# Merging four stages of a macaron network into one pipeline over sequences, with the weights rounded during the stage before

## The chip, the cores and the metric

The kernel runs on one core of one Trainium2 chip. Its time is the device time of that core in microseconds (us), from the start of the program to its end. A core has five engines with instruction queues of their own: TensorE (PE, matrix products), VectorE (DVE), ScalarE (ACT), GpSimd (POOL) and SyncE (SP, which here issues the transfers). Each works its queue off in order, and semaphores tie the queues together.

## The reference

A residual network of four layers works on 8 sequences of 512 tokens with 128 features, all in fp32. Each layer has a half-weighted feed-forward, a mixer and the same feed-forward again. The stretch that matters here is layer 2 and the first third of layer 3:

```python
x = x + 0.5 * _L1_ffn_ref(_layernorm(x), ...)   # mixture of 16 experts, 4 of them used
x = x + 0.5 * _L2_ffn_ref(_layernorm(x), L2_ffn_w_gate, L2_ffn_w_up, L2_ffn_w_down)
x = x + _L2_attn_ref(_layernorm(x), L2_attn_ig_w, ..., L2_attn_a_param)
x = x + 0.5 * _L2_ffn_ref(_layernorm(x), L2_ffn_w_gate, L2_ffn_w_up, L2_ffn_w_down)
x = x + 0.5 * _L3_ffn_ref(_layernorm(x), L3_ffn_w1, L3_ffn_b1, L3_ffn_w2, L3_ffn_b2)
x = x + _L3_attn_ref(_layernorm(x), ...)        # causal attention, 16 heads
```

The feed-forward of layer 2 rounds inputs, weights and hidden values to a 4-bit grid, with one scale for each 16 values:

```python
def fp4_quant_dequant(x):                       # blocks of 16 along the last dimension
    scale = maximum(max(abs(xb)) / 6, 1e-12)    # one for each block
    return grid[searchsorted(mid, abs(xb / scale))] * sign(xb) * scale
gate = fp4_linear(x, w_gate); y = fp4_linear(x, w_up)      # 128 -> 352
return fp4_linear(silu(gate) * y, w_down)                  # 352 -> 128
```

The mixer of layer 2 is a linear recurrence over the tokens, with gates `sigmoid(block-diagonal product)`:

```python
log_a = -8 * gate_a * softplus(a_param)
normed_x = x * gate_x * sqrt(clip(1 - exp(2 * log_a), 1e-7))
p = clip(shifted cumprod(exp(log_a)), 1e-7)     # along the tokens
h = p * cumsum(normed_x / p)
```

The feed-forward of layer 3 is `relu(x @ w1 + b1) @ w2 + b2` with 512 hidden values.

## The kernel before

The residuals stay in SBUF for the whole program, as eight tiles `x0` to `x7` of 128 partitions (tokens) by 4 chunks by 128 features. The program is a list of twelve stages (`_STAGES`, L1595), and `_run_stages` (L1612) calls one after the other. Each stage opens its own pools in SBUF and PSUM, loops over the sequences, and ends with the residual add of each (`add_half`, L391, or L1140 in the recurrence). A framework orders the instructions of each engine by priorities that follow the order of emission, subject to the buffers: pools of a stage take the space that the stage before gives back. The exception is the norm: its tiles come from `ln_pool`, which lives for the whole program, so that norms can be made ahead over a stage's border. Weights come by DMA from SP, one packed transfer for a stage (`load`, L261).

The parts that the change touches:

- `norm` (L274) makes the statistics (`bn_stats` L282, `bn_aggr` L283 on DVE), then one over the root by `pow` on POOL (L285, L287), then applies it, either on ACT (L291 and L293, `scalar=True`) or on DVE (L298). `transposed` (L377) turns four chunks on PE (L381) and copies them from PSUM by ACT (L382).
- `fp4` (L967) rounds a tile. DVE finds the largest value of each block (L977), makes the scale and its inverse (L978, L980, L981). POOL multiplies by the inverse (L983). ACT makes a large number of the same exponent (L985), by which DVE rounds in two passes (L986, L987). POOL multiplies by the scale (L988). One such chain goes DVE, POOL, ACT, DVE, POOL.
- `l2_ffn` (L990) rounds and transposes the three weights the first time it runs (copies at L1008 and L1015), then goes over the sequences: `rounded_in` (L1032: norm, rounding, transposition), `gated_half` (L1041) twice, of two token chunks each (products `pg` and `pu`, silu by ACT L1053, product by DVE L1054, rounding), and `rounded_half` (L1058), one half later (transposes L1066, copies by ACT L1067, product `po` with the down weights, add). The stage runs twice.
- `l2_attn` (L1084) makes the softplus of its rate, then goes over all eight sequences three times: norm, transposition and gates (sigmoid L1112, product by POOL L1113); decay (exponential L1116, POOL L1117, DVE L1118, scaling by the rate L1120, a running sum with a floor as a scan L1123, two exponentials L1126 and L1127); and sums (root L1130, POOL L1131, DVE L1133, scan L1135, product L1136, transposes L1139, add L1140). Changes between sigmoid, exponential, root and silu on ACT cost a table load each.
- `l3_ffn` (L1142) has for each sequence norm (apply on DVE), transposition, four products of 128 by 512 with relu on ACT (L1167), four more that add up in PSUM, bias on ACT (L1176), transposes back (L1158) and add.
- `l1_ffn` (L794), the stage ahead, steps through the experts of each sequence in ten steps (`experts`, L853) and takes the routing of the next sequence along (`routed` L821; `ranks` L897, with POOL's comparison at L910). Its shares, transposed as `shareT`, weigh the experts' products. A generator `self.aside` is stepped at each of the ten steps of sequence 1; in the first of the two expert stages it makes constants of the attention. `in_order` (L331) fixes the order of the named engines within a step as it was written.

In all of them `mm` (L272) is the line of every matrix product.

Of the kernel before, what the change touches and what calls it, by code (L numbers as in the profile page):

```python
# [10 lines left out]

# [14 lines left out]
P = 128  # L26
# [175 lines left out]
def _attention_pack(p, wq, bq, wk, bk, wv, bv, wo, bo):  # L202
# [32 lines left out]
    ),  # L235
}


class _Kernel:
# [554 lines left out]
    def l1_ffn(self):  # L794
# [3 lines left out]
        with ExitStack() as s:  # L798
# [10 lines left out]
            for b in range(NB):  # L809
                ahead = self.routed(b + 1) if b + 1 < NB else iter(())  # L810
                experts = self.experts(b)
                for _ in range(10):
                    with self.in_order(*(() if b != 1 else (mybir.EngineType.Pool, mybir.EngineType.DVE))):
                        next(experts)
                        next(ahead, None)
                        if b == 1:
                            next(self.aside, None)
                for _ in ahead:
                    pass
# [147 lines left out]
    def fp4(self, out, v, sb, tag):  # L967

        nc = self.nc
        n = v.shape[1]
        blocks = lambda ap: ap.rearrange("p (k i) -> p k i", i=16)
        spread = lambda ap: ap.unsqueeze(2).to_broadcast([P, n // 16, 16])
        scale = sb.tile([P, n // 16], F32, name=f"{tag}_scale")
        nc.vector.tensor_reduce(scale, blocks(v), AX.X, ALU.max, apply_absolute_value=True)  # L977
        nc.vector.tensor_scalar(scale, scale, 1.0 / 6.0, 1e-12, ALU.mult, ALU.max)  # L978
        inv = sb.tile([P, n // 16], F32, name=f"{tag}_inv")
        nc.vector.reciprocal(inv, scale)  # L980
        nc.vector.tensor_scalar(inv, inv, 2.0**-23 - 1.0, None, ALU.mult)  # L981
        r = sb.tile([P, n], F32, name=f"{tag}_r")
        nc.gpsimd.tensor_tensor(blocks(r), blocks(v), spread(inv), ALU.mult)  # L983
        big = sb.tile([P, n], F32, name=f"{tag}_big")
        nc.scalar.activation(big, r, AF.Abs, scale=2.0**22)  # L985
        nc.vector.scalar_tensor_tensor(r, big, 1.5 * 2.0**22, r, ALU.max, ALU.add)  # L986
        nc.vector.scalar_tensor_tensor(r, big, 1.5 * 2.0**22, r, ALU.max, ALU.subtract)  # L987
        nc.gpsimd.tensor_tensor(blocks(out), blocks(r), spread(scale), ALU.mult)  # L988

    def l2_ffn(self):  # L990
        nc, tc = self.nc, self.tc
        w = lambda n: self.w["l2f", n]
        F = 352
        chunk = self.l2_chunks = [(0, P), (P, P), (2 * P, F - 2 * P)]
        with ExitStack() as s:
            sb = s.enter_context(tc.tile_pool(name="sb", bufs=2))
            ps = s.enter_context(tc.tile_pool(name="ps", bufs=2, space=bass.MemoryType.PSUM))
            if not self.l2w:

                self.load("l2f")  # L1000
                for name in ("w_gate", "w_up"):
                    q = sb.tile([P, 3 * P], F32, name="wq")
                    self.fp4(q, w(name), sb, "w")
                    pt = ps.tile([P, 3 * P], F32, name="mm", bufs=1)
                    for k in range(3):
                        nc.tensor.transpose(pt[:, bass.ts(k, P)], q[:, bass.ts(k, P)], self.ident)
                    self.l2w[name] = self.const.tile([P, F], F32, name=f"{name}T")
                    nc.vector.tensor_copy(self.l2w[name], pt[:, :F])  # L1008
                q = sb.tile([P, F], F32, name="wq")
                self.fp4(q, w("w_down"), sb, "w")  # L1010
                self.l2w["w_down"] = self.const.tile([P, 3, P], F32, name="w_downT")
                pt = ps.tile([P, 3, P], F32, name="mm", bufs=1)
                for k, (at, n) in enumerate(chunk):
                    nc.tensor.transpose(pt[:n, k, :], q[:, at : at + n], self.ident)
                    nc.vector.tensor_copy(self.l2w["w_down"][:n, k, :], pt[:n, k, :])  # L1015


            self.sb, self.ps = sb, ps
            self.seqs = [{} for _ in range(NB)]
            self.rounded_in(0)  # L1020
            last = None
            for b in range(NB):
                for half in range(2):
                    self.gated_half(b, half)
                    if last is not None:
                        self.rounded_half(*last)
                    last = (b, half)
                    if half == 0 and b + 1 < NB:
                        self.rounded_in(b + 1)
            self.rounded_half(*last)  # L1030

    def rounded_in(self, b):  # L1032
        sb, ps = self.sb, self.ps
        flat = "p c d -> p (c d)"
        xn = self.norm(self.x[b], self.ln_pool, scalar=True)
        xq = sb.tile([P, NC, D], F32, name="xq")
        self.fp4(xq.rearrange(flat), xn.rearrange(flat), sb, "x")
        xT = sb.tile([P, L], F32, name="xT")
        self.seqs[b]["xT"] = self.transposed(xq, ps, xT, self.nc.scalar.copy, bufs=1)

    def gated_half(self, b, half):  # L1041
        nc, sb, ps = self.nc, self.sb, self.ps
        q, wT = self.seqs[b], self.l2w
        F = 352
        flat = "p c d -> p (c d)"
        h = sb.tile([P, 2, F], F32, name="h")
        for j in range(2):
            tok = q["xT"][:, bass.ts(2 * half + j, P)]
            pg = ps.tile([P, F], F32, name="pg")
            self.mm(pg, tok, wT["w_gate"])  # L1050
            pu = ps.tile([P, F], F32, name="pu")
            self.mm(pu, tok, wT["w_up"])
            nc.scalar.activation(h[:, j, :], pg, AF.Silu)  # L1053
            nc.vector.tensor_tensor(h[:, j, :], h[:, j, :], pu, ALU.mult)  # L1054
        q[half] = sb.tile([P, 2, F], F32, name="hq")
        self.fp4(q[half].rearrange(flat), h.rearrange(flat), sb, "h")

    def rounded_half(self, b, half):  # L1058
        nc, sb, ps = self.nc, self.sb, self.ps
        q, hq = self.seqs[b], self.seqs[b][half]  # L1060
        if half == 0:
            q["hT"] = sb.tile([P, 3, L], F32, name="hT")
        for k, (at, n) in enumerate(self.l2_chunks):
            pt = ps.tile([P, 2, P], F32, name="ht")
            for j in range(2):
                nc.tensor.transpose(pt[:n, j, :], hq[:, j, at : at + n], self.ident)  # L1066
            nc.scalar.copy(  # L1067
                q["hT"][:n, k, bass.ts(half, 2 * P)], pt[:n].rearrange("p c t -> p (c t)")
            )
        if half == 0:  # L1070
            return
        po = ps.tile([P, NC, P], F32, name="po", bufs=1)
        for c in range(NC):
            for k, (_, n) in enumerate(self.l2_chunks):
                self.mm(
                    po[:, c, :],
                    q["hT"][:n, k, bass.ts(c, P)],
                    self.l2w["w_down"][:n, k, :],
                    start=k == 0,
                    stop=k == 2,  # L1080
                )
        self.add_half(b, po)

    def l2_attn(self):  # L1084

        nc, tc = self.nc, self.tc
        w = lambda n: self.w["l2a", n]
        with ExitStack() as s:  # L1090
            keep = s.enter_context(tc.tile_pool(name="keep", bufs=1))
            sb = s.enter_context(tc.tile_pool(name="sb", bufs=2))
            ps = s.enter_context(tc.tile_pool(name="ps", bufs=2, space=bass.MemoryType.PSUM))
            floor = keep.tile([P, L], F32, name="floor")
            nc.gpsimd.memset(floor, float(np.log(1e-7)))
            ones = keep.tile([P, L], F32, name="ones")
            nc.gpsimd.memset(ones, 1.0)
            rate = keep.tile([P, 1], F32, name="rate")
            self.softplus(rate, w("a_param"), keep)
            nc.vector.tensor_scalar(rate, rate, -8.0, None, ALU.mult)  # L1100
            rate2 = keep.tile([P, 1], F32, name="rate2")
            nc.vector.tensor_scalar(rate2, rate, 2.0, None, ALU.mult)

            gated, decay, left, prefix = [], [], [], []
            for b in range(NB):
                xn = self.norm(self.x[b], self.ln_pool, scalar=True)
                xT = self.transposed(xn, ps, sb.tile([P, L], F32, name="xT"), nc.scalar.copy)
# [491 lines left out]
    "l1_ffn",  # L1599
    "l1_attn",  # L1600
    "l1_ffn",
    "l2_ffn",
    "l2_attn",
    "l2_ffn",
    "l3_ffn",
# [32 lines left out]
```

## Time and profile before

| what | value |
|---|---|
| time, median of 3 runs | 2497.51 us (2494.47 to 2501.63) |
| the profiled execution's own time | 2500.23 us |
| its span | 2498.4 us |
| mean granted TensorE clock | 0.902 |
| TensorE busy | 2142.6 us (86%) |
| VectorE busy | 1665.3 us (67%) |
| ScalarE busy | 1216.5 us (49%) |
| GpSimd busy | 652.5 us (26%) |

The shares are means over twelve stages with different limits; what the change is worth has to be read in its own stretch, from the last residual add of the second expert stage to that of layer 3's first feed-forward. In the lines by group, a row gives line, engine, operation, output and inputs, count, then the busy time in us and the mean of one in ns, then the idle time of the engine ahead of it and what ended it. In the waits, a row gives the engine and line that waited, what it waited for, the total in us, how often, and the longest. In the windows, a row gives the stretch, its length, each engine's busy time with the number of instructions, and the granted clock. In the slices a digit is the busy share of one fortieth of the span, in tenths.

### The profile page before, as it was taken

To read this page: it belongs to the slowest core of one execution; us is meant where nothing else is said; L and a number is where in the kernel's file an instruction comes from. 1 tells how busy PE (TensorE), PEld (TensorE's weight loads), DVE (VectorE), ACT (ScalarE), POOL (GpSimd) and SP (SyncE) were. 2 spreads that over 40 slices of the span, in tenths; PEclk is the share of its full clock that TensorE was granted. 3 is DMA by queue.
4 is the path that set the end of the run, shared out by engine and by line. 5 is a ranking of instruction groups with operands and counts; after the bars stand their busy time and mean duration, and the time that the engine had idled before them with its cause. 6 is when DMAs were issued, how large, how long until landed. Compare 5 with 4: busy or idle time off the path is not lost.

```text
span 2498.4 us, 30167 instructions
## 1 busy us (share of the span) xinstructions
PE 2142.6 (86%) x10907; PEld 1033.5 (41%) x10967; DVE 1665.3 (67%) x3867; ACT 1216.5 (49%) x1791; POOL 652.5 (26%) x922
## 2 busy tenths in 40 slices
PE   7679998889998988899979996762578999999989
PEld 3444444434444333333334443541354444444434
DVE  4566774568768788888358777957884466666611
ACT  3545663323321666777723333455444335555554
POOL 1123443012111011112112114553552113333330
PEclk9779998989996899999979998975888969999999
DMA  3000000000000000000000000000000000000001
GB/s 117 1 1 1 1 1 13 10 0 1 0 1 0 1 1 1 1 1 1 1 7 0 1 1 0 1 1 0 1 1 1 0 1 1 1 1 1 1 1 34
DMA packets 10036, 13.08 MB, mean 5 GB/s; under 512 B 416, under 2 KB 8736, under 8 KB 9760
## 3 DMA queue, kind: packets, MB, share of 16 engines
q1 hardware_dynamic: 7776, 10.11, 1.2%
q8 instruction: 86, 1.41, 0.2%
q10 hardware_dynamic: 2112, 1.05, 0.2%
q14 instruction: 62, 0.51, 0.1%
HBM read 9.06 MB, written 2.10 MB: 4 GB/s over the span
## 4 chain that ended last, share of the span: by engine, by line
PE 63%; DVE 19%; POOL 7%; ACT 7%; issue 4%; DMA 0%; ACTq 0%; DVEq 0%; SPq 0%; POOLq 0%
PE pair L272 11%; PE av L272 8%; PE po L272 7%; PE first L272 7%; PE mm L272 6%; PE pg L272 5%; PE pu L272 4%; DVE max L1393 3%; ACT e L1501 3%; PE ph L272 2%; PE ck L272 2%; PE pr L272 1%; PE pw L272 1%; POOL xn_rstd L287 1%; DVE xn L298 1%
## 5 line engine op out<-in xcount | busy, mean ns | idle before, releaser
L1393 DVE TENSOR_REDUCE max<-first 128x1 f32<-128x512 f32 (+3 forms) x864 | 534.8, 666 | 193.5 <-PE first L272 170.4
L1501 ACT ACTIVATE e<-pair 128x1024 f32<-128x1024 f32 (+3 forms) x512 | 436.8, 865 | 241.7 <-PE pair L272 231.4
L272 PE MATMUL first<-qkT 32*128 32x512 f32 (+3 forms) x1024 | 338.4, 474 | 30.6 <-DVE max L1393 29.4
L272 PE MATMUL pair<-qkT 32*128 32x512 f32 (+3 forms) x1024 | 224.3, 457 | 21.1 <-ACT e L1501 14.3
L272 PE MATMUL av<-e,v 128*32 128x512 f32 (+3 forms) x2048 | 240.2, 539 | 1.0
L872 ACT ACTIVATE act<-pg 128x512 f32<-128x512 f32 x144 | 86.0, 597 | 235.1 <-PE pg L272 188.1
L272 PE MATMUL pair<-mT,max_rows 32*128 32x512 f32 (+3 forms) x1024 | 192.1, 376 | 1.8 <-DVE mT L1435 1.8
L272 PEld LDWEIGHTS pair<-qkT 32*128 32x128 f32 x1024 | 95.8, 186 | 235.4 <-ACT e L1501 132.7
L272 PEld LDWEIGHTS first<-qkT 32*128 32x128 f32 x1024 | 153.1, 198 | 96.3 <-DVE max L1393 87.8
L1503 POOL TENSOR_SCALAR_AFFINE_SELECT e<-e 128x256 f32<-128x256 f32 x256 | 103.4, 407 | 253.1 <-ACT e L1501 252.8
L272 PE MATMUL po<-act,w_moe 128*128 128x512 f32 x288 | 157.4, 632 | 3.0 <-DVE act L881 1.9
L272 PE MATMUL pg<-xT,w_moe 128*128 128x512 f32 x288 | 153.7, 616 | 0.0
L272 PE MATMUL pu<-xT,w_moe 128*128 128x512 f32 x288 | 149.3, 601 | 0.0
L873 DVE TENSOR_TENSOR act<-act,pu 128x512 f32<-128x512 f32 x144 | 98.3, 683 | 49.6 <-PE pu L272 47.3
L1399 POOL COPY copies<-max 128x128 f32<-128x128 f32 x64 | 22.6, 410 | 343.3 <-DVE max L1393 343.3
L272 PEld LDWEIGHTS pair<-mT,max_rows 32*128 32x128 f32 x1024 | 97.4, 189 | 3.6 <-DVE mT L1435 3.3
L881 DVE TENSOR_TENSOR act<-act,pw 128x512 f32<-128x512 f32 x128 | 87.1, 682 | 16.5 <-PE pw L272 15.0
L287 POOL TENSOR_TENSOR xn_rstd<-xn_rs,nhalf 128x4 f32<-128x4 f32 x72 | 77.5, 1077 | 54.1 <-ACT xn L293 35.5
L382 ACT COPY xT<-mm 128x512 f32<-128x512 f32 x80 | 46.0, 584 | 89.0 <-PE mm L381 76.8
L381 PE MATMUL mm<-w_const,xn 128*128 128x128 f32 x256 | 51.4, 318 | 42.2 <-DVE xn L298 24.8
L1360 ACT CAST qkT<-pair 128x1024 fp32r<-128x1024 f32 x64 | 64.8, 1014 | 41.3 <-PE pair L272 40.8
L910 POOL TENSOR_TENSOR ge<-ge,w_moe 128x64 f32<-128x64 f32 (+1 forms) x32 | 42.8, 1337 | 153.8 <-DVE ge L908 153.8
(354 smaller groups left out, 4211.2 us busy)
## 6 DMA issues: line engine op xcount, KB each, us to landing
w_moe<-in_moe SPq DMA_DIRECT2D x1, 2392.0 KB, 13.7
out<-x SPq DMA_DIRECT2D x8, 256.0 KB, 2.3
x<-in_u ACTq DMA_DIRECT2D x4, 256.0 KB, 6.5
x<-in_u SPq DMA_DIRECT2D x4, 256.0 KB, 6.4
w_mixer<-in_l0a SPq DMA_DIRECT2D x1, 960.5 KB, 8.2
w_mixer<-in_l1a SPq DMA_DIRECT2D x1, 769.0 KB, 4.2
w_ffn<-in_l0f SPq DMA_DIRECT2D x1, 578.0 KB, 7.3
w_ffn<-in_l2f SPq DMA_DIRECT2D x1, 560.0 KB, 3.5
```

What stands on the lines that cost most here:

```text
L272: self.nc.tensor.matmul(out, lhsT, rhs, start=start, stop=stop)
L287: nc.gpsimd.tensor_tensor(rstd, rs, self.nhalf[:, :n], ALU.pow)
L381: self.nc.tensor.transpose(pt[:, c, :], xn[:, c, :], self.ident)
L382: copy(out, pt.rearrange("p c t -> p (c t)"))
L872: nc.scalar.activation(act, pg, AF.Silu)
L873: nc.vector.tensor_tensor(act, act, pu, ALU.mult)
L881: nc.vector.tensor_tensor(act, act, pw[e % 2], ALU.mult)
L910: nc.gpsimd.tensor_tensor(ge.rearrange(flat), ge.rearrange(flat), self.wide(before, m), ALU.mult)
L1360: self.nc.scalar.copy(t, p)
L1393: nc.vector.tensor_reduce(mx[:, c, j, gs[0] : gs[-1] + 1], sc, AX.X, ALU.max, negate=True)
L1501: nc.scalar.activation(e[:, :, :n], sc[:, :, :n], AF.Exp, scale=scale)
L1503: nc.gpsimd.affine_select(e[:, :, :P], e[:, :, :P], pattern=[[0, 2], [1, P]], compare_op=ALU.is_ge, fill=0.0, base=0, channel_multiplier=-1,)
```

## The change

The four stages `l2_ffn`, `l2_attn`, `l2_ffn` and `l3_ffn` become one, `layer2`. Each sequence's work in each of them is cut into pieces, and every piece has a slot, a number that only orders them. A sequence b's first rounded feed-forward lies at 5.5 b, its recurrence, which goes by pairs of sequences, at 7 + 8 b for the odd b, its second rounded feed-forward at 32 + 8 b, and its relu feed-forward at 40 + 8 b. The pieces are emitted by rising slot.

```diff
+_STARTS = (0, 7, 32, 40)
+_STEPS = (5.5, 8, 8, 8)
+_ROUNDED_FFN = {
+    "stats": -9, "apply": -5, "x_in": -5, "x_out": -4, "turned": -1.5,
+    "gated": (0.5, 0.5, 1, 1), "h_in": (0.5, 2.5), "h_out": (2, 4),
+    "h_turned": (3.5, 5), "down": 7,
+}
+_RECURRENCE = {
+    "stats": -1, "apply": 2, "turned": 2, "gates": 3.5, "decays": 4, "exps": 4,
+    "roots": 4.5, "sums": 5.5, "added": 6.5,
+}
+_RELU_FFN = {
+    "stats": 0.5, "apply": 0.5, "turned": 2, "wide": (3.5, 3.5, 4, 4), "product": 5.5, "added": 10,
+}
...
+    def layer2(self):
...
+            for b in range(NB):
+                put(_STEPS[0] * b, self.rounded_ffn(b))
+                put(_STEPS[2] * b + _STARTS[2], self.rounded_ffn(b))
+                put(_STEPS[3] * b + _STARTS[3], self.relu_ffn(b))
+                if b % 2:
+                    put(_STEPS[1] * b + _STARTS[1], self.recurrence((b - 1, b)))
+            for _, piece in sorted(todo, key=lambda t: t[0]):
+                piece()
```

PSUM has two banks each of `pg`, `pu` and `mm`, which the kinds of piece share, and one each of `ht` and `po`. The norms (`front`) take their tiles from the stage's pool and are all applied on ACT:

```diff
+        def stats():
+            st = sb.tile([P, NC, 6], F32, name=f"{tag}_st")
...
+            nc.gpsimd.tensor_tensor(t["rstd"], rs, self.nhalf[:, :NC], ALU.pow)
+        def apply():
...
+            nc.vector.scalar_tensor_tensor(off, mv[:, :, 0], -1.0, rstd, ALU.mult, ALU.mult)
+            for c in range(NC):
+                nc.scalar.activation(xn[:, c, :], x[:, c, :], AF.Identity, ...)
```

The rounding is cut in two pieces, works in place, and two of its small instructions take a tile of constants as a second input:

```diff
-        nc.vector.tensor_scalar(scale, scale, 1.0 / 6.0, 1e-12, ALU.mult, ALU.max)
+        nc.vector.scalar_tensor_tensor(
+            scale, scale, 1.0 / 6.0, self.least[:, :m], ALU.mult, ALU.max
+        )
...
-        nc.vector.tensor_scalar(inv, inv, 2.0**-23 - 1.0, None, ALU.mult)
-        r = sb.tile([P, n], F32, name=f"{tag}_r")
+        nc.vector.tensor_tensor(inv, inv, self.below[:, :m], ALU.mult)
+        r = sb.tile([P, n], F32, name=f"{tag}_r", bufs=bufs)
...
-        nc.gpsimd.tensor_tensor(blocks(out), blocks(r), spread(scale), ALU.mult)
+        nc.gpsimd.tensor_tensor(self.blocks(r), self.blocks(r), self.each(scale), ALU.mult)
```

The recurrence runs its scan on the unscaled gate, with a limit divided by the rate, and scales in the exponentials; the clip of one minus the square joins POOL's instruction:

```diff
-                nc.gpsimd.tensor_scalar(t, t, -1.0, 1.0, ALU.mult, ALU.add)
-                nc.vector.tensor_scalar(t, t, 1e-7, None, ALU.max)
...
-                nc.vector.tensor_scalar(decay[b], decay[b], rate, None, ALU.mult)
+                nc.gpsimd.tensor_scalar(q["left"], q["left"], 1.0, -1e-7, ALU.subtract, ALU.min)
...
+                    p[:, 1:], q["ag"][:, : L - 1], self.limit[:, : L - 1], 0.0, ALU.add, ALU.min
...
+                nc.scalar.activation(q["ag"], q["p"], AF.Exp, scale=self.minus)
+                nc.scalar.activation(q["p"], q["p"], AF.Exp, scale=self.rate)
...
+                nc.scalar.activation(q["left"], q["left"], AF.Sqrt, scale=-1.0)
```

The softplus, the constants and the rounding and transposition of the three weights go into a generator, `layer2_constants`, which the second expert stage steps at steps 3 and 8 of its first seven sequences; there the order within the steps is not fixed. Its first part, with the weights' transfer, runs ahead of that stage:

```diff
-                for _ in range(10):
-                    with self.in_order(*(() if b != 1 else (mybir.EngineType.Pool, mybir.EngineType.DVE))):
+                ordered = self.aside_at[0] if b == 1 else ()
+                for step in range(10):
+                    with self.in_order(*ordered):
                         next(experts)
                         next(ahead, None)
-                        if b == 1:
+                        if (b, step) in self.aside_at[1]:
                             next(self.aside, None)
...
+        if at == 5:
+            k.aside = k.layer2_constants(ctx)
+            next(k.aside)
+            k.aside_at = (), [(b, n) for b in range(NB - 1) for n in (3, 8)]
```

## The prediction

> **What bounds the kernel now.** I read the page's slices first, then windows cut at the stage borders, then the waits inside them, then groups by line and form. Borders are the last residual add of each stage: 1518.0 us (second expert stage), 1665.5, 1751.1, 1898.3, 1966.5. The slices (62.5 us each) locate the weak stretch at slices 25 to 31:
>
> ```profile
> PE   7679998889998988899979996762578999999989
> DVE  4566774568768788888358777957884466666611
> ```
>
> The windows give each engine's busy time per stage: the experts, then weight rounding with the first norm, the first rounded feed-forward, the recurrence, the second rounded feed-forward, the relu feed-forward, and the last five together:
>
> ```profile
> core 0: us, PE busy (x) PEld busy (x) DVE busy (x) ACT busy (x) POOL busy (x), PEclk, DMA share, GB/s
> 1270.00:1518.00 248.00, 237.13 (x643) 102.39 (x641) 183.34 (x509) 79.67 (x127) 43.72 (x57) 0.97 0.01 2
> 1518.00:1538.60 20.60, 4.29 (x13) 2.24 (x13) 19.05 (x51) 7.41 (x18) 13.12 (x13) 0.53 0.00 0
> 1538.60:1665.50 126.90, 90.94 (x444) 63.92 (x444) 107.10 (x232) 56.53 (x133) 69.29 (x60) 0.88 0.00 1
> 1665.50:1751.10 85.60, 31.50 (x96) 16.56 (x96) 52.84 (x91) 53.46 (x87) 34.38 (x36) 0.64 0.00 0
> 1751.10:1898.30 147.20, 96.65 (x448) 69.52 (x448) 121.60 (x315) 64.06 (x145) 82.92 (x76) 0.81 0.00 1
> 1898.30:1966.50 68.20, 65.78 (x195) 32.37 (x196) 23.42 (x106) 32.07 (x48) 10.73 (x17) 0.95 0.00 1
> 1518.00:1966.50 448.50, 289.16 (x1196) 184.61 (x1197) 324.00 (x790) 213.53 (x430) 210.44 (x201) 0.81 0.00 1
> ```
>
> No engine is busy for the 448.5 us: VectorE (DVE) comes nearest with 324. The stages have different limits. DVE is 83 to 84% busy in the rounded feed-forwards, nothing is over 62% in the recurrence, and TensorE (PE) is 96% busy in the relu feed-forward while DVE idles two thirds of it. The waits say who is late:
>
> ```profile
> ACT hT L1067 <- PE ht L1066: 65.5, 42, 5.9
> PEld ht L1066 <- POOL hq L988: 52.4, 30, 6.4
> PE mm L1139 <- DVE h L1136: 46.0, 7, 25.3
> DVE x L391 <- PE back L1158: 38.4, 8, 5.8
> POOL hq L988 <- DVE h_r L987: 27.0, 16, 3.3
> ```
>
> TensorE waits on the rounding chain and on the scans, DVE waits on the relu products: work that only a border keeps apart. The rows of the costs (busy us, mean ns):
>
> ```profile
> L986 DVE SCALAR_TENSOR_TENSOR h_r<-h_big,h_r 128x704 f32<-128x704 f32 x32 | 35.3, 1103 | 10.0 <-ACT h_big L985 9.9
> L988 POOL TENSOR_TENSOR hq<-h_r,h_scale 128x704 f32<-128x704 f32 x32 | 44.6, 1394 | 61.5 <-DVE h_r L987 27.0 <-DVE h_inv L981 10.0 <-PE pg L272 9.9
> L298 DVE TENSOR_SCALAR xn<-x,xn_mv,xn_rstd 128x128 f32<-128x128 f32 x32 | 10.5, 382 | 9.3 <-PE mm L381 6.2 <-POOL xn_rstd L287 3.1
> L978 DVE TENSOR_SCALAR h_scale<-h_scale 128x44 f32<-128x44 f32 x32 | 13.4, 419 | 0.0
> L291 DVE SCALAR_TENSOR_TENSOR xn_off<-xn_mv,xn_rstd 128x4 f32<-128x4 f32 x19 | 7.3, 383 | 19.1 <-POOL xn_rstd L287 19.1
> L1126 ACT ACT_TABLE_LOAD x2 | 2.6, 1283 | 0.0
> ```
>
> **The change, part by part.**
>
> *Removed and added work.* DVE: 324.0 in the region. Weight rounding leaves it (lines 977 to 987 on the three weights and the copies 1008 and 1015: 9.6) with softplus (2.2): −11.8. Lines 1118 and 1120 go: −8.4. The relu norm's apply (L298) goes to ScalarE: −10.5. Left: 293.3, and 8 `off` instructions of 0.16 to 0.38 come: 295. ScalarE (ACT): 213.5, plus 32 applies at 486 ns (L293's row) = 15.6, plus table loads. The built program has 16 in the region against 11 (sigmoid, exponential, root and silu for each of four pairs): 5 × 1.28 = 6.4; less 1.7 for weights and softplus: about 234. GpSimd (POOL): 210 less 6 for weights, 205. PE: 289.2 less 3.1 for the nine weight transposes.
>
> *A rule weighed.* The trace shows a load as 1283 ns, the last activation ending 0.02 us before it and the next beginning 0.01 after. The Trainium skill (ScalarE: Activation LUTs, What ACT_TABLE_LOAD costs) adds 1380 ns of drain to each change of set, 2.66 us in all; it speaks against more changes. By the rule ACT would hold 16 × 1.38 = 22 more, 256, still under DVE, and the root's load in the three bare pairs below would add 4 us. No drain is visible here, so I take the row.
>
> *Holds on DVE.* I split the region's DVE instructions by whether POOL worked at that time: L986 takes 879 ns alone and 1238 beside POOL, L978 175 and 663, L291 161 and 582; over the region this comes to about 45 us. The change turns L978 and L981 (19 us of the 45) into two-input forms. Bounds: −19 if these escape, 0 if not; L291 is a small two-input form and is held alike, so 0. POOL's share rises from 47% to about 56%, which could raise 45 by a fifth (+9) or, where the order parts them, not at all: I take +5. DVE: 300.
>
> *Overlap.* In the new stage DVE's order mixes rounding, recurrence and relu pieces of different sequences, so the bound is DVE's 300 plus what is bare. PE (286, less at a higher granted clock: 0.81 here, 0.97 in the experts) lies beside it; from slot 46 on, where second feed-forward and relu overlap, my share-out of the windows' busy times over the pieces gives 134 us for DVE and 147 for PE: nearly level. Bare pieces:
> - Start. The norm's tiles now belong to the stage and cannot be made ahead. Statistics (4 × 0.43), `pow` 1.04, four applies, then reduce, product 1.1, ACT 0.63, two passes, product 1.16, transposes, copy: about 15 us to the first gate, with DVE idle for 8.
> - Recurrence pairs. A scan, two exponentials, a table load, the root and POOL's 1.7 us product must pass before L1133's counterpart. In the first, third and fourth pair only small DVE instructions stand between: 3 × 5 = 15.
> - Tail. The last sequence is serial: after its last rounding 7 us to the residual add (transposes, copies, 2.6 of `po`, 0.69), then a relu feed-forward alone: statistics and `pow` 3, applies 1.9, transposes and copy 1.7, eight products of 0.86, bias 0.69, transposes 1.1, add 0.69, some 17. Of these 24 DVE works 3: +21. In before this tail was one sequence of a PE-bound stage.
> - Between pieces. Before's rounded feed-forwards leave 16% of DVE bare with one stage's work at hand; here two or three sequences are. I take 5% (15); bounds 3% and 16%.
>
> 300 + 8 + 15 + 21 + 15 = 359, against 448.5: −89.5. PSUM's `ht` falls from two banks to one, so a transpose waits for the copy before it (0.37 us); other matmuls stand between these in PE's order, so 0; bare they would cost 16 × 5 × 0.4 = 32 on PE, which stays near DVE.
>
> *Into the experts.* 11.8 us of DVE go where DVE is busy for 183 of 248: covered, except at the stage's start. There PE has 21.4 of 28 us busy (1272 to 1300) as it awaits the first routing. Now about 13 small instructions (softplus, scales) stand ahead of the routing on DVE, and two POOL products of 0.85 and one more before the `ge` of L910 (2.35 us); that chain feeds `shareT`, without which the expert products can't begin. Sum: 2 to 4 on DVE, 3 to 4 on POOL. Nine transposes on a PE 98% busy: 1.5. I take +8, from +4 (the idle PE time takes half) to +14 (each step waits a POOL turn more). SP's order is unchanged, the layer's weights load at the same place in it: 0. POOL's two memsets there are under 1 us.
>
> Sum: −89.5 + 8 = −81.5. The profiled execution took 2500.2, 2.7 above the median of the three runs (span 2498.4 and 1.8 around it); 2500.2 − 81.5 = 2418.7, and against the median 2416.
>
> **The rivals.**
> - *The queues fill each other* and DVE is nearly always fed: 295 + 8 + 5 + 17 + 9 (3%) and +4 in the experts: 338, −110: 2387. For: the mix has three independent kinds of work. Against: ACT, POOL and DVE run in order, and a late piece holds the next.
> - *The chains stay half bare.* 48 chains (16 × 3) cross DVE, POOL, ACT, DVE, POOL. Before left (126.9 − 107.1)/24 = 0.8 and (147.2 − 121.6)/24 = 1.1 us of idle DVE for each. If 1.2 stays: 300 + 8 + 15 + 21 + 58 = 402, +8: −38, 2459.
> - *Slower: POOL's queue in order becomes the pacemaker.* A product of one chain queues behind other sequences' products (1.4) and the recurrence's (1.0 to 1.7), ACT waits for it, DVE behind ACT. It turns slower when each of the 48 chains leaves (448.5 − 8 − 344)/48 = 2.0 us of DVE bare, twice today's. At 2.6: +29, 2526. Against: POOL has only 205 us of work.
> - *The border stays:* if the pieces ran in effect one stage after the other, 2497. The built order mixes them, so I give it 2%.
>
> **How the numbers follow.** Forecast 0.57, queues filled 0.22, half bare 0.15, pacemaker 0.04, no effect 0.02. Faster 0.94, same 0.02, slower 0.04; about 0.3% (7.5 us) is what a measurement can tell from no change. Unknowns at their good ends (no holds added, 5 in the pairs, 3%, +4) give about 2380; at their bad ends (holds 310, pairs 20, tail 24, 13% bare, experts 14) 310 + 8 + 20 + 24 + 40 + 14 = 416, −32, about 2465. The range 2378 to 2460 takes in the two faster rivals and leaves out the last and the far ends.
>
> **What would show it.** Right: a merged stage of about 360 us with DVE over 80% busy in it; gate matmuls begin about 15 us after the expert stage's last add; two-input counterparts of L978 and L981 near 400 ns in the mean; bare DVE before L1133's counterpart in three of four pairs; the last relu alone for some 17 us; the experts' stage about 8 us longer, at its start. Wrong: DVE under 75% with waits on POOL's rounding products; PE the busier engine; the expert stage longer by over 14; or small instructions at 160 ns, which would shift the DVE sum by up to 19.

## The result and the profile after

The changed kernel took 2483.59 us in the median (2481.17 to 2484.66), the kernel before 2497.61 beside it: a ratio of 0.9942, 95% interval 0.9924 to 0.9959. It is faster, by 14 us where 81 were forecast, and outside the forecast range. The profiled execution took 2481.17 us, 19.1 less than that of before. By the last residual add of each stage, in both traces:

| stretch | before | after | difference | forecast |
|---|---|---|---|---|
| start to the end of the first expert stage | 752.1 | 749.7 | -2.4 | 0 |
| attention of layer 1 | 518.0 | 527.8 | +9.8 | 0 |
| second expert stage | 247.9 | 251.3 | +3.4 | +8 |
| the four stages, then the merged one | 448.1 | 418.1 | -30.0 | -89.5 |
| attention of layer 3, last feed-forward | 529.0 | 529.2 | +0.2 | 0 |

Two numbers want an explanation: why the merged stage is 418 and not 359, and why the attention of layer 1, which the change does not touch, is 10 us longer. The slices of the page after:

```profile
PE   7679998889998989888869997776778899999989
DVE  4566774568768788888547776879677465666611
```

The weak stretch (slices 25 to 31) is more even than before, but TensorE (PE) and VectorE (DVE) mostly stay at 6 to 8 tenths in it. The windows of the changed kernel give the start up to the first gate product, the part with most of the first feed-forwards and two recurrence pairs, the part with the other two pairs and most of the second and relu feed-forwards, the last 18 us, and the whole:

```profile
core 0: us, PE busy (x) PEld busy (x) DVE busy (x) ACT busy (x) POOL busy (x), PEclk, DMA share, GB/s
1528.80:1546.80 18.00, 1.87 (x8) 1.46 (x9) 14.40 (x63) 8.01 (x19) 10.48 (x15) 0.55 0.00 0
1546.80:1713.00 166.20, 115.51 (x476) 77.69 (x474) 137.88 (x298) 96.32 (x196) 102.64 (x87) 0.77 0.00 1
1713.00:1913.10 200.10, 153.96 (x625) 93.02 (x623) 147.27 (x378) 119.01 (x236) 109.21 (x97) 0.91 0.00 1
1928.60:1946.90 18.30, 11.88 (x24) 4.94 (x24) 3.21 (x15) 5.67 (x10) 1.87 (x3) 0.81 0.00 0
1528.80:1946.90 418.10, 295.73 (x1184) 184.25 (x1184) 310.74 (x769) 235.93 (x472) 230.49 (x205) 0.84 0.00 1
```

DVE works 310.7 us (forecast 300) and is bare for 107.4 (forecast 59). The named pieces of bare time were no larger than forecast: 18.0 - 14.4 = 3.6 at the start (forecast 8), 15.1 in the last 18.3 us and 5.4 just ahead of them at the tail (forecast 21), and the recurrence pairs in the second of these waits:

```profile
DVE x L431 <- PE po L312: 18.2, 9, 6.2
DVE ag L1283 <- POOL ig L1280: 12.9, 3, 5.2
DVE a_off L1143 <- POOL a_rstd L1137: 10.0, 7, 2.4
DVE f_off L1143 <- POOL f_rstd L1137: 9.9, 9, 1.5
DVE h_r L1036 <- ACT big L1035: 8.2, 16, 1.7
DVE r_off L1143 <- POOL r_rstd L1137: 7.3, 8, 1.1
```

Three stalls of 12.9 us together stood against three of 5. What is left, 107.4 - 3.6 - 20.5 - 12.9 = 70 us, is bare time between the pieces, where the forecast had 15. It is spread over many short waits, and from 1713 to 1913 neither engine is near its bound: DVE works 147 and PE 154 of 200 us. The experiments look for what paces this stretch.

### The profile page after: what moved, and what is told of

The parts are those of the page before. It is cut to its first block, busy times and chain, and to the rows that moved or that the text cites. A ratio compares the mean times of both kernels' runs of the same rounds, so it can differ in the third digit from the quotient of the medians.

```text
span 2479.4 us, 30103 instructions
## 1 busy us (share of the span) xinstructions
PE 2147.4 (87%) x10907; PEld 1031.0 (42%) x10967; DVE 1657.7 (67%) x3830; ACT 1235.7 (50%) x1828; POOL 671.0 (27%) x923
## 4 chain that ended last, share of the span: by engine, by line
PE 61%; DVE 20%; POOL 9%; ACT 6%; issue 4%; DMA 0%; ACTq 0%; DVEq 0%; SPq 0%; POOLq 0%
PE pair L312 10%; PE av L312 8%; PE first L312 7%; PE po L312 7%; PE mm L312 6%; PE pg L312 5%; PE pu L312 5%; DVE max L1590 4%; ACT e L1698 2%; PE ck L312 2%; PE pr L312 1%; PE pw L312 1%; PE ph L312 1%; PE pi L312 1%; PE pf L312 1%
## 5 line engine op out<-in xcount | busy, mean ns | idle before, releaser
L312 PE MATMUL pair<-qkT 32*128 32x512 f32 (+3 forms) x1024 | 223.6, 455 | 19.6 <-ACT e L1698 13.1
L922 DVE TENSOR_TENSOR act<-act,pw 128x512 f32<-128x512 f32 x128 | 87.0, 681 | 15.6 <-PE pw L312 13.8
L1198 PE MATMUL ht<-w_const,h_r 128*128 128x128 f32 (+1 forms) x192 | 47.8, 339 | 53.6 <-POOL h_r L1038 29.4
L312 PEld LDWEIGHTS pu<-xT,w_moe 128*128 128x128 f32 x288 | 53.6, 192 | 63.8 <-issue 59.0
L421 PE MATMUL mm<-w_const,xn 128*128 128x128 f32 x192 | 39.7, 323 | 41.7 <-DVE xn L338 26.0
## 6 DMA issues: line engine op xcount, KB each, us to landing
w_moe<-in_moe SPq DMA_DIRECT2D x1, 2392.0 KB, 14.2
```

The source lines that it names most:

```text
L312: self.nc.tensor.matmul(out, lhsT, rhs, start=start, stop=stop)
L421: self.nc.tensor.transpose(pt[:, c, :], xn[:, c, :], self.ident)
L922: nc.vector.tensor_tensor(act, act, pw[e % 2], ALU.mult)
```

## The experiments

Each kernel is the changed one with the main lines of its edit shown (`...` stands for lines left out); times are ratios to the kernel before. A word on what such a run can show: the framework arranges each engine's instructions anew for every kernel. Matching the sequences in the traces, I find that DVE's in the merged stage is more than 99% the same as in the change with the fixed order, 86% without POOL's product (noscale), 81% in forms, 73% without the relu work, and about 60% in roots and ht_banks (instructions that an edit adds or removes set aside). Where the order moved that far, the time shows the edit and the new order together.

**The attention of layer 1.** The old second expert stage fixed the order of POOL (GpSimd) and DVE in the steps of sequence 1; the change keeps this for the first expert stage alone.

```diff
-            k.aside_at = (), [(b, n) for b in range(NB - 1) for n in (3, 8)]
+            k.aside_at = (mybir.EngineType.Pool, mybir.EngineType.DVE), [(b, n) ...]
```

> The second expert stage gets back the fixed order of POOL and DVE within the steps of sequence 1, nothing else is changed. Theory: without that order the norms of sequences 2 to 6 are queued into layer 1's attention, which is why it takes 527.8 us instead of 518.0; with the order they go back behind it, attention 518 +-2, expert stage 248 to 256, whole about 2475 against 2483.6. Rival: the attention is longer for another reason (placement of tiles, the earlier weights), then it stays near 528 and the whole within 3 us of 2483.6.

Measured: 2479.72 us, ratio 0.9930 (0.9915 to 0.9944). The attention took 518.2 us, the expert stage 254.9, the merged stage 417.4. The windows of that attention before, after and with the order fixed:

```profile
752.10:1270.10 518.00, 460.26 (x3022) 193.46 (x3023) 390.53 (x746) 325.60 (x349) 76.19 (x98) 0.91 0.00 1
```
```profile
749.70:1277.50 527.80, 461.01 (x3023) 193.76 (x3024) 397.44 (x796) 325.85 (x350) 81.99 (x109) 0.91 0.00 1
```
```profile
747.80:1266.00 518.20, 458.70 (x3023) 193.48 (x3024) 392.66 (x751) 324.45 (x348) 77.00 (x101) 0.91 0.00 1
```

After, DVE has 50 instructions more in it. Forty of them are the expert norms (20 statistics, 16 aggregations, 4 applications), whose tiles come from the pool that lives for the whole program; the other ten, about 4 us, are of the softplus and the weights' rounding. Rows of before, after and fixed order over the whole attention:

```profile
L282 DVE BATCH_NORM_STATS2 xn_st<-x 128x6 f32<-128x128 f32 x8 | 2.0, 274 | 4.6 <-POOL x L1574 4.6
```
```profile
L322 DVE BATCH_NORM_STATS2 xn_st<-x 128x6 f32<-128x128 f32 x28 | 6.9, 273 | 18.0 <-POOL x L1771 18.0
```
```profile
L322 DVE BATCH_NORM_STATS2 xn_st<-x 128x6 f32<-128x128 f32 x8 | 2.0, 273 | 4.6 <-POOL x L1771 4.6
```

The 20 statistics more cost 5 us of work and 13 us more of waiting: at the head of DVE's queue they wait for POOL's residual add, and the attention's maxima behind them are late. PE's waits for these maxima, in the same order, show it:

```profile
PE first L272 <- DVE max L1393: 25.7, 60, 1.7
```
```profile
PE first L312 <- DVE max L1590: 35.7, 65, 3.7
```
```profile
PE first L312 <- DVE max L1590: 27.5, 60, 1.7
```

They grew by 10 us, as the attention did, and fell back by 8. All runs here without the fixed order have an attention of 527.7 to 531.2 us, all with it 515.3 to 518.8. The theory holds; the fixed order also keeps about half of the ten other instructions out, but DVE does not stand still before those. The whole gained less than 10 us, because the expert stage is 3.6 longer and the last two stages of that execution were slower by 5.6; the intervals of this kernel and of the change overlap.

**The weights, without the move.**

```diff
-            k.aside_at = (), [(b, n) for b in range(NB - 1) for n in (3, 8)]
+            k.aside_at = (mybir.EngineType.Pool, mybir.EngineType.DVE), []
...
+        with ExitStack() as s:      # ahead of the pipeline, in pools of its own
+            self.sb, self.ps = ...
+            for _ in self.aside:
+                pass
```

> The weights, the softplus and the constants are made at the start of the merged stage instead of during the experts, in pools of their own that are given back before the pipeline starts; the expert stage has its fixed order and nothing else besides. Theory: the move into the experts saved about what the weights took before (20.6 us, 8 to 12 of it shared with the first norm) and costs 3 to 7 there: attention 518, expert stage 248, merged stage 434 to 444, whole 2486 to 2498. Rival: the move is worth nothing, since the first norm's chain takes as long as the weights: merged stage under 425, whole 2472 to 2480.

Measured: 2483.81 us, ratio 0.9948 (0.9929 to 0.9966): the time of the change. The expert stage took 248.2 us, the merged stage 430.4, between what the theory and its rival expected (its profiled execution took 2497.66, the longest of its runs, so that number may be some us high). The move is worth at most about 12 in the merged stage and costs 3 to 7 in the experts. In the change as made, the norms in the attention cost what was left of it.

**How much overlap there is.** Two runs frame it: the old stages one after the other in the emitted order, and the emitted order enforced on four engines, which the framework otherwise rearranges by its own estimates.

```diff
-_STARTS = (0, 7, 32, 40)
-_STEPS = (5.5, 8, 8, 8)
+_STARTS = (0, 80, 180, 280)
+_STEPS = (8, 8, 8, 8)
```

> The merged stage with starts 0, 80, 180, 280 and step 8: the four old stages one after the other in the emitted order, all other parts of the change kept. Theory: the 30 us that the stage gained are overlap, and the rest of the change costs (norms tied to the stage, pairs, five table loads): merged stage 455 to 480 us, whole 2520 to 2545. Rival: the overlap gives little and the gain comes from the weights rounded earlier and the shorter recurrence: merged stage 420 to 440, whole 2485 to 2505.

```diff
+            E = mybir.EngineType
+            with self.in_order(E.PE, E.DVE, E.Activation, E.Pool):
                 for _, piece in sorted(todo, key=lambda t: t[0]):
                     piece()
```

> PE, DVE, ACT and POOL keep, within the merged stage, the order in which the pieces were emitted; in the change the framework reorders by its own estimates. If the slots' own order is what fails to overlap, the same 418 within 10. If the reordering had mended it, longer: 430 to 480. If the reordering had spoiled it, shorter than 405.

Measured: 2632.93 us (1.0541, 1.0525 to 1.0557), merged stage 562.1; and 2738.39 (1.0955, 1.0927 to 1.0984), merged stage 672.8. Both are far beyond what I expected. The window of the serial kernel over seven sequences of the first feed-forward shows why:

```profile
1583.40:1751.10 167.70, 99.70 (x400) 74.89 (x398) 105.16 (x208) 61.10 (x119) 71.04 (x54) 0.72 0.00 0
```

That is 24.0 us a sequence with DVE at 63%, where the old stage took 126.9/8 = 15.9 with DVE at 84%. Cut by the residual adds, the serial kernel's first feed-forward with its start takes 213.9 us (before, with the weights, 147.4), its recurrence 85.5 (85.6), the second feed-forward 188.5 (147.2) and the relu feed-forward 74.2 (68.2): 108 of the 114 us that it loses against before lie in the rounded feed-forwards. The old code put one half's transposes between the next half's gates; cut into pieces that lie 8 slots apart, one sequence hardly overlaps the next. That this is the cause is argued from the code, since the serial kernel also has the other parts of the change (norms tied to the stage, one `ht` bank, rounding in place), and it sets the first feed-forward's step to 8 where the change has 5.5. By this measure the merge wins 562 - 418 = 144 us by overlap, after the cutting had lost 562 - 448 = 114. My sum started from the old stages' density and saw only the winning side. The strict kernel shows that the slots are only a part of the schedule: in exactly the emitted order the stage is 255 us longer than in the order that the framework makes of it.

**What paces the later part.** Its last rounded feed-forwards end 25.5, 21.9 and 21.4 us apart, about what one takes alone. First, the work of PE: the relu pieces left out altogether.

```diff
-                put(_STEPS[3] * b + _STARTS[3], self.relu_ffn(b))
```

> The relu feed-forward's pieces are left out of the merged stage (its part of the computation is missing: about 66 us of PE, 32 of ACT and 18 of DVE), all else as in the change. Theory of the chain (the later part of the stage is paced by one sequence's way through gates, rounding, transposes and down product, about 24 us a sequence, and the relu work lies in its gaps): only its serial tail of some 17 us and little more goes, merged stage 393 to 402. Theory of the work (PE and DVE together have too much to do): merged stage 375 or less.

Measured: ratio 0.9874 (0.9857 to 0.9890).

```profile
1533.50:1929.90 396.40, 237.03 (x992) 166.95 (x992) 305.16 (x688) 194.51 (x392) 221.08 (x189) 0.73 0.00 1
```

With 59 us less of PE and 41 less of ACT the stage is 21.7 shorter, little more than the serial tail, and the last feed-forwards end 30.1, 24.4 and 21.3 us apart, no closer. The lower granted clock (0.73, after 0.84) does not hide a gain: a gate product took 513 ns in the mean against 516. So the amount of PE's work does not pace the stage.

Second, buffers and waits that the lists of waits offer: three PSUM banks shared by `ht` and `mm`; transposes and down product later; the offset made by POOL, so that DVE need not wait for the root.

```diff
-                pt = self.ps.tile([P, 2, P], F32, name="ht", bufs=1)
+                pt = self.ps.tile([P, NC, P], F32, name="mm", bufs=3)[:, :2]
...
```

> The transposes of the hidden values take their PSUM bank from the three that then serve ht and mm together, so that one need not wait for the copy of the one before. Theory of the single bank: the 24 us that PE and the 41 us that its weight loads wait for ACT's copies lie on the path: merged stage shorter by 10 or more, whole 2473 or less. Theory of the coupled order (PE waits for rounding, DVE for gates, whichever bank): within 4 us of 2483.6.

```diff
-_STARTS = (0, 7, 32, 40)
+_STARTS = (0, 10, 34, 44.5)
-    "h_turned": (3.5, 5), "down": 7,
+    "h_turned": (9.25, 9.75), "down": 10.5,
...
```

> Transposes and down product of a sequence are emitted after the next sequence's gate products (slots 9.25, 9.75 and 10.5 in place of 3.5, 5 and 7, the later starts moved to 10, 34 and 44.5, buffers shared out anew). Theory of the coupled order: the 62 us of DVE idle time between pieces come from PE standing at transposes while DVE rounds and DVE standing while PE makes transposes, down product and gates; with a sequence more between them the merged stage falls from 418 to 385 to 403, whole 2450 to 2468. Rival: DVE stands for POOL's roots and ACT's copies as often in this order: merged stage within 6 of 418, or longer by the longer fill.

```diff
+            nc.gpsimd.tensor_tensor(off, mv[:, :, 0], t["rstd"], ALU.mult)
+            nc.gpsimd.tensor_scalar(off, off, -1.0, None, ALU.mult)
...
-            nc.vector.scalar_tensor_tensor(off, mv[:, :, 0], -1.0, rstd, ALU.mult, ALU.mult)
```

> The norm's offset (mean times root, negated) is made by POOL in two instructions behind the root, in place of one on DVE, so that DVE no longer stands at the head of its queue for POOL's root. Theory of the in-order wait (27 us of DVE's waits in the stage are offset for root): merged stage shorter by 12 to 25, 393 to 406. Theory of the chain: DVE would have stood for something else, within 5 of 418; POOL has 15 us more to do, so a few us longer is possible.

Measured: 2508.68 (1.0046, 1.0031 to 1.0061), 2513.26 (1.0066, 1.0046 to 1.0085) and 2501.22 (1.0010, 1.0001 to 1.0020), with merged stages of 439.5, 445.6 and 428.0 us. All three are longer; all three expectations of a gain failed, and for ht_banks the rival's "within 4 us" as well. The order changed in all of them, and the second also shares its buffers out anew (two for hidden values and inputs in place of three, five for rounded hidden values), so they show only that none of the edits helps as made. The third is instructive all the same, by DVE's waits:

```profile
DVE x L431 <- PE po L312: 29.4, 14, 7.0
DVE ag L1285 <- POOL ig L1282: 19.9, 4, 7.2
...
DVE h L1185 <- ACT h L1184: 14.2, 9, 2.2
DVE h_r L1036 <- ACT big L1035: 12.9, 13, 2.4
```

The 27 us of offset for root are gone, and the other waits took their place (18.2 became 29.4, 12.9 became 19.9, 2.2 became 14.2, 8.2 became 12.9). DVE works 6 us less and stands bare for 16 us more (123 against 107). So this wait in the list was not a loss that could be had back by this edit. The likely reading is that DVE waited there for a chain that was late in any case, and that 17 us more for POOL made it later; the new order may have its part in it, and no run parts the two.

Third, the chain's own length. POOL's second product of the hidden values is left out, and they go on unscaled:

```diff
-        nc.gpsimd.tensor_tensor(self.blocks(r), self.blocks(r), self.each(scale), ALU.mult)
+        if r.shape[1] != 704:
+            nc.gpsimd.tensor_tensor(self.blocks(r), self.blocks(r), self.each(scale), ALU.mult)
```

> POOL's second product of the hidden values' rounding (32 times 1.57 us, 50 us in all) is left out, so the hidden values go on unscaled; DVE, ACT and PE keep their work. Theory that POOL's steps lie on the chain that paces the stage: 32 steps of 1.57, half of them or more bare: merged stage shorter by 25 to 50. Theory that DVE's and PE's queues pace each other and POOL's steps are hidden: shorter by less than 10.

Measured: ratio 0.9823 (0.9798 to 0.9848), merged stage:

```profile
1533.20:1916.70 383.50, 278.40 (x1184) 174.17 (x1184) 292.24 (x770) 235.70 (x474) 180.15 (x173) 0.88 0.00 1
```

It is 34.6 us shorter. DVE, whose instructions are the same, works 18.5 us less, and its bare time falls by 16, from 107.4 to 91.3. Most of the 18.5 is time for which POOL held DVE: what DVE's instructions beside POOL take beyond the median of the same ones alone, the prediction's split, sums to about 45 us in the change and 30 here. The 16 of bare time are what POOL's steps on the chain and the changed order make together.

Fourth, more sequences side by side. Two tries:

```diff
-_STARTS = (0, 7, 32, 40)
-_STEPS = (5.5, 8, 8, 8)
+_STARTS = (0, 7, 42.5, 50.5)       # step6
+_STEPS = (5.5, 8, 6, 6)
+_STARTS = (0, 8.5, 29.5, 37.5)     # even55
+_STEPS = (5.5, 5.5, 5.5, 5.5)
```

> The second rounded feed-forward and the relu feed-forward go by 6 slots a sequence in place of 8 and start at 42.5 and 50.5 in place of 32 and 40, with the fixed order in the expert stage kept (its effect is known: attention 518, expert stage 255). Theory of the chain: with a step of 8 one sequence's pieces (0.5 to 7) hardly overlap the next one's; at 6 gates of the next come ahead of the down product, the period falls from 24.6 us to 21, merged stage 395 to 408. Rival: what the shorter step gains is lost to the later start: 412 to 425.

> All four kinds of piece go by 5.5 slots a sequence, with starts 0, 8.5, 29.5 and 37.5, the earliest that the residuals allow, with the fixed order in the expert stage kept. Theory of the chain: more streams of different sequences lie side by side for longer, DVE over 80% busy, merged stage 380 to 405. Rival: with two rounded feed-forwards in flight the three buffers of a kind and the two PSUM banks run out, and queues in order collide: 418 or longer.

In both, slots tie, so that the second feed-forward of sequence 6 (step6) or of each even sequence (even55) reads its residual ahead of the recurrence's add; their times bear on a work with fewer dependences. Measured: 2488.15 (0.9957, 0.9944 to 0.9971) with a merged stage of 433.0, and 2466.81 (0.9870, 0.9855 to 0.9886) with 407.4. The first lies beyond its rival's range and the second between the two ranges. A shorter step with a later start loses. Then the even steps with the order of the residuals kept, and denser:

```diff
+_STARTS = (0, 8.5, 29.75, 37.75)   # even55b
+_STEPS = (5.5, 5.5, 5.5, 5.5)
+_STARTS = (0, 8.5, 28.75, 36.75)   # even45
+_STEPS = (4.5, 4.5, 4.5, 4.5)
```

> All four kinds of piece by 5.5 slots a sequence with starts 0, 8.5, 29.75 and 37.75, so that every second feed-forward is emitted after the add of its recurrence, and the fixed order kept in the expert stage. Theory of the chain (a sequence's way through the rounding paces the stage unless other sequences are in flight): merged stage 400 to 412, whole 2462 to 2472. Rival: each pair's recurrence now truly stands between, with less room than at 8 slots: merged stage 418 or more, whole 2478 or more.

> As even55b, with 4.5 slots a sequence and starts 0, 8.5, 28.75 and 36.75. Theory of the chain (more sequences in flight hide more of it): merged stage 385 to 400, whole 2442 to 2456. Rival: at three buffers of a kind no more sequences fit, further ones wait for space: 402 or longer.

Measured: 2459.02 (0.9831, 0.9806 to 0.9855) and 2458.90 (0.9848, 0.9829 to 0.9867), merged stages 403.5 and 403.0. The window of the first:

```profile
1525.50:1929.00 403.50, 294.46 (x1184) 185.30 (x1184) 305.62 (x768) 240.85 (x477) 221.01 (x205) 0.85 0.00 1
```

The even steps of 5.5 with their earlier starts bring 14 us against the 417.4 with the same fixed order, 3 of them in the tail after the last rounded feed-forward (15.1 against 18.3); 4.5 in place of 5.5 brings nothing, as its rival had it. Does POOL still pace this order? Its product is left out again, and in another run the recurrence's clip goes from POOL to DVE:

> As even55b, with POOL's second product of the hidden values left out (they go on unscaled). In the change the same edit took 34.6 us off the merged stage, 18.5 of them by DVE instructions that POOL no longer held, 16 by idle DVE. Theory that POOL's steps still pace the denser order: 403.5 falls by 28 to 40. Theory that with more sequences in flight the steps are hidden: by 10 to 22, which is the hold alone.

```diff
-                nc.gpsimd.tensor_scalar(q["left"], q["left"], 1.0, -1e-7, ALU.subtract, ALU.min)
+                nc.vector.tensor_scalar(q["left"], q["left"], 1.0, -1e-7, ALU.subtract, ALU.min)
```

> As even55b, with the recurrence's clip (POOL, 8 times 2.0 us) made by DVE (about 0.4 us each, 4 in all). Theory that POOL's queue paces the stage: merged stage 3 to 12 shorter than 403.5, whole 2447 to 2456. Rival that DVE's queue does: within 3, or up to 4 longer.

```profile
1518.00:1906.80 388.80, 282.95 (x1184) 178.44 (x1184) 291.81 (x768) 242.49 (x479) 173.15 (x173) 0.87 0.00 1
```

Without the product the stage is 14.7 us shorter and DVE's work 13.8; the bare time stays, 97.9 and 97.0 (DVE's sequence is 90% the same). With the clip on DVE (2457.52 us, 0.9843, 0.9818 to 0.9868) the stage is 402.4, the same, in nearly the same order (99%) and with 14.5 us less on POOL. So with more sequences in flight POOL's steps are hidden, and what POOL still costs is that it holds DVE. That supports the way of one sequence, not POOL's queue, as what paced the order of the change; it does not prove it, since no run lengthens or shortens that way alone.

**The small instructions of the rounding.**

```diff
-            scale, scale, 1.0 / 6.0, self.least[:, :m], ALU.mult, ALU.max
+        nc.vector.tensor_scalar(scale, scale, 1.0 / 6.0, 1e-12, ALU.mult, ALU.max)
-        nc.vector.tensor_tensor(inv, inv, self.below[:, :m], ALU.mult)
+        nc.vector.tensor_scalar(inv, inv, 2.0**-23 - 1.0, None, ALU.mult)
```

> The two small instructions of each rounding are tensor_scalar again, without the second input tile. Theory that both forms are held by POOL alike: their four rows together 31 to 40 us (31.3 in the change, 35.8 before), merged stage within 5 of 418. Rival, that the two-input forms escape part of the hold: rows 40 us or more, merged stage 424 or longer.

Measured: 2488.16 us (0.9950, 0.9932 to 0.9968), merged stage 415.3. The hidden values' rows of the change, and of this kernel:

```profile
L1025 DVE TENSOR_TENSOR h_inv<-h_inv,below 128x44 f32<-128x44 f32 x32 | 11.5, 360 | 0.1
L1018 DVE SCALAR_TENSOR_TENSOR h_scale<-h_scale,least 128x44 f32<-128x44 f32 x32 | 9.2, 288 | 0.0
```
```profile
L1023 DVE TENSOR_SCALAR h_inv<-h_inv 128x44 f32<-128x44 f32 x32 | 14.4, 449 | 0.2
L1018 DVE TENSOR_SCALAR h_scale<-h_scale 128x44 f32<-128x44 f32 x32 | 8.4, 263 | 0.0
```

With the input's rows the sums are 31.3 and 34.2 us: 3 us apart, where an escape was put at 9 or more. One row is longer and one shorter with the second input, so neither form escapes: in the change, L1025 takes 193 ns in the mean where POOL does not work beside it and 574 where it does.

## Why the prediction was wrong, by its own steps

- *"Between pieces: I take 5% (15); bounds 3% and 16%"* is the term that failed: it measured 70 us, 23% of DVE's work. I took before's 16% as the worst and divided it by three because two or three sequences would be at hand. (The 16% is a share of the stretch; as a share of DVE's work, like the 5%, it is 19.8/107.1 = 18%, and the 70 us lie beyond that bound too.) The step that was wrong is to start from the density of the old stages: that belonged to their code, which the cutting gave up, and the new pieces one sequence after the other leave 37% of the stretch bare. More sequences at hand win most of that back, not more. The half-bare rival, 402 us for the stage, was nearest, and still 16 too low.
- *DVE 300* was 310.7, and not by holds: counted alike in both traces they come to about 49 us before (the prediction had 45) and 45 after, so "+5" did not come. Work was left out of the sum. The prediction says at *Start* that the norms cannot be made ahead any more, but it does not count them: before, the statistics of seven sequences (28 instructions) ran in the expert stage, so that the four stages' norms had 100 in the stretch where the merged stage has 128.

```profile
L282 DVE BATCH_NORM_STATS2 xn_st<-x 128x6 f32<-128x128 f32 x100 | 25.4, 270 | 0.0
```
```profile
L1132 DVE BATCH_NORM_STATS2 f_st<-x 128x6 f32<-128x128 f32 x64 | 16.2, 266 | 0.1
L1132 DVE BATCH_NORM_STATS2 a_st<-x 128x6 f32<-128x128 f32 x32 | 8.0, 268 | 0.0
L1132 DVE BATCH_NORM_STATS2 r_st<-x 128x6 f32<-128x128 f32 x32 | 8.0, 271 | 0.1
```

That is 6.8 us. The offsets are 13 more, not 8 (7.3 us before, 13.1 after, against 1.7 in the sum), and the recurrence's scan with the new limit took 14.6 us in place of 11.0. 295 + 6.8 + 4.1 + 3.6 = 309.5. POOL had 230 us, not 205, 8 of them for a reason below.

- *Into the experts, +8, "the order within the steps" at nothing.* The experts cost 3.4, which is luck: the norms that had gone into the attention were missing there, and with the order fixed the cost is 254.9 - 247.9 = 7.0. I had listed that the fixed order goes, and never asked what it had held back: the norms of five sequences, 10 us in a stage that I did not look at. That they were moved past the attention's maxima could have been read from the built order on DVE and POOL.
- *Start 8, pairs 15, tail 21* measured 3.6, 12.9 and 20.5; the first gate came after 18 us, not 15, and the last relu feed-forward took 18, not 17. From 1745 us on, about where slot 46 falls, DVE has 131 us of work and PE 152, forecast 134 and 147. `ht` in one bank at 0: more banks did not help.
- *The two-input forms at 0* against -19: held (forms).
- *Table loads at 1283 ns:* 16 rows of 1283 ns in the stage; in the trace after, the next activation mostly begins 11 ns behind a load, so no drain shows there either, and with ACT at 236 of 418 us none was near the bound.
- *Slower by POOL's queue:* it did not come to that. Of that rival the half seems true that POOL's steps lay on the path (noscale).
- *The signs.* "DVE under 75%" came true (310.7 of 418.1 is 74%), but not DVE's waits on POOL's rounding products: for these it was PE's transposes that waited (29.4 us) and ACT (16.4).

The forecast's sum from the stage's terms: 10.7 more work and 48.4 more bare time make the stage 59 us longer than forecast; the attention adds 9.8, the experts give back 4.6, and the other stages give back 2.2.

What stays open: why the pieces leave 70 us bare is shown only in part. Overlap of more sequences moves it (14 us by the even steps), POOL's product moves it in the order of the change, and PE's relu work does not. With 5.5 slots DVE is still bare for 98 us. Of these, leaving out POOL's product took less than 1; space for more sequences was not tried apart from the step, and the framework's order was not held fixed in these runs.

## What to carry to other kernels

When stages with an order of their own are cut into pieces for a pipeline, first ask what the pieces take with nothing beside them; overlap has to pay that back before it gains. And count the work that stages had done ahead in their neighbours: it comes back. A wait high in the list need not be a loss that can be had back: here one was removed and four grew. And when an ordering constraint is dropped, look through the whole program for what it kept out, above all for work in pools that outlive a stage.

## What the runs showed of the hardware

The recurrence's clip was joined to POOL's instruction as (subtract, min) in place of (multiply, add), same shape, and I costed that at nothing. The rows before and after:

```profile
L1117 POOL TENSOR_SCALAR left<-left 128x512 f32<-128x512 f32 x8 | 8.1, 1020 | 10.8 <-ACT left L1116 10.8
```
```profile
L1262 POOL TENSOR_SCALAR left<-left 128x512 f32<-128x512 f32 x8 | 16.3, 2034 | 0.7
```

The fastest of the eight took 779 ns before and 1917 after, where seven of the eight lie between 1917 and 1928, so it is the operations and not a hold; on DVE the same instruction took 410 ns at the least (even_left). In most of the profiled executions one to four sequences of the last attention took about 54.5 us where the others took 51.5, at changing places; nothing here explains it, and it is a reason not to read 3 us from one trace.
